# Another list of how many of a step's sums are taken by twos, in a graph-network layer on one core

## The chip, the cores and the metric

The kernel runs on one core of one Trainium2 chip. Its time is the device time of one execution in microseconds; lower is better. A core has a matrix engine (TensorE: PE for its matmuls, PEld for its weight loads), a vector engine (VectorE, DVE), a scalar engine (ScalarE, ACT), GpSimd (POOL) and SyncE (SP), which issues most of the transfers here.

## The reference

The layer normalises nodes, adds up the edges that arrive at each node, and puts both through a two-layer perceptron with a residual. There are N = 12,500 nodes of 128 numbers and 412,500 edges of 48 numbers, sorted by the node that they arrive at.

```
h = maximum(layernorm(x), 0)
agg = segment_sum(edge_attr_48, dst, num_segments=12500)
hid = relu(concat([h, agg, u]) @ W1 + b1)      # u: one row, the same for all nodes
out = x + hid @ W2 + b2
```

All is float32.

## The kernel before, in words

**Edges.** A chunk is 896 edges, 7 on each of 128 partitions, so an edge's number t on its partition runs from 0 to 6. A step takes 8 chunks, in two halves h of 4 chunks; there are 58 steps, the last a shorter one. `load` (L297) fetches two chunks at a time, 336 KB, on SP's queue; `few` (L290) lets five loads be under way and ties a load to TensorE's last issued product. 18 tiles hold edges.

**Sums.** Since the edges are sorted, a chunk's edges arrive at few neighbouring nodes, and its sums go to a window of W = 32 columns. `onehot` (L308) makes on DVE, for a whole step, ones where an edge's node is that of the column. `aggregate` (L334) multiplies: a *position* is one t of one half, so a step has 14 positions. A position can be taken in two ways, and both give the same sums:

- singly: four products, one for each chunk of the half, each with 32 columns of ones as weights and 48 numbers moving through, into 32 partitions of the bank `ps`;
- by twos: two products, each with the 64 columns of two neighbouring chunks as weights and the 96 numbers of both chunks moving through. Half of what that makes (one chunk's ones with the other chunk's edges) is of no use and is never read.

Each product in float32 is two matmuls and two weight loads in the trace. `LEVELS[s]` (L608) says for each step s how many of its 14 positions are taken by twos; L886 deals them out, the second half first and from its last position backwards, so that a step with a level of 1 to 13 begins with single positions and changes once to twos. Where a half has twos, the sums of odd chunks lie 48 numbers further in the bank, and `keep_sums` (L355) copies them on ACT with two more, narrow copies beside the wide one.

**Placing.** `place_columns` (L372, DVE) and `place` (L378, PE, bank `pp`) spread a step's sums over the nodes of its stretch, and `add` (L386, DVE) adds them to `aggT`, two steps after the sums (one step after in the last seven, `LATE`).

**Nodes.** 26 blocks of up to 512 nodes go through `stats`, `root`, `factors`, `normal` (DVE and ACT), `turn` and `keep` (transposed on PE, copied on ACT), `first_h` and `first_a` (first layer, bank `ph`, L468 and L493), `relu` (ACT, tile `hid`, L508), `second` (second layer, bank `po`, L518), `result` (DVE, L527) and `store`. The first five blocks (`FIRST`) are begun early; their half results are kept and added later by `add_h` (L482, DVE). POOL adds the last bias to x (`plus_b2`, L428), clears `aggT` and issues most stores.

**Order.** All is issued by hand, step by step. In step s the loads of step s + 3 go out, then come the pieces of block work that a small planner has given to the step (`piece`, L707), the place of step s − 2, the 14 positions of step s, its copies, its place columns and the ones of step s + 2. The planner does not read `LEVELS`.

Of the kernel before, what the change touches and what calls it, by code (L numbers as in the profile page):

```python
# [22 lines left out]
def kernel(  # L23
# [134 lines left out]
    with fast:  # L158
# [175 lines left out]
        def aggregate(s, h, twos):  # L334
            left = s == NSF and h
            if h == 0:
                banks_s[s] = ps_agg.tile([P, 512], F32, name="ps")[:, :4 * DE].rearrange("p (h f) -> p h f", h=2)
            ps, es, oh = banks_s[s], edges[s], onehots[s]
            n = TT if left else T
            for t in range(n):  # L340
                first, end = t == 0 and h == 0, t == n - 1
                if t >= n - twos:
                    for q in range(0, CH, 2):
                        c = CH * h + q
                        product(ps[W * q:W * (q + 2), h], oh[:, c // 2, t], both[s][c // 2][:, :, t * DE:(t + 1) * DE],
                                start=first, stop=end, skip_group_check=True)
                    continue
                for q in range(1 if left else CH):
                    c = CH * h + q
                    o = DE * (q % 2) if twos else 0  # L350
                    product(
                        ps[W * q:W * (q + 1), h, o:o + DE], oh[:, c // 2, t, c % 2], es[c][:, t * DE:(t + 1) * DE],
                        start=first, stop=end, skip_group_check=True)
# [32 lines left out]
        def add(s):  # L386
            _, v = nc.values_load_multi_w_load_instructions(  # L387
                at_i[0:1, s:s + 1], engines=[DVE], min_val=low(s), max_val=high(s),
                skip_runtime_bounds_check_because="clamped to these on the chip")
            to = aggT[:HI + DE, ds(v[0], WG)]  # L390
            nc.vector.tensor_tensor(to, to, banks_p.pop(s)[:HI + DE, :WG], OP.add)  # L391
# [213 lines left out]
        FLIGHT = 5  # L605


        LEVELS = (0, 0, 0, 0, 7, 0, 0, 9, 14, 3, 14, 14, 0, 14, 3, 3, 2, 0, 5, 14, 0, 14, 2, 3, 0, 4, 14, 0, 14, 2, 4, 0, 3, 0, 5, 14, 0, 14, 0, 4, 0, 2, 0, 3, 14, 0, 14, 4, 2, 2, 0, 2, 2, 4, 0, 0, 0, 0)  # L608
        LATE = NS - 7
        NEAR = len(FIRST) + 1  # L610
        with tc.manual_schedule():
# [242 lines left out]
            for s in range(NS):  # L854
# [27 lines left out]
                if s >= LATE:  # L882
                    for p in now:
                        place(p)
                        add(p)
                twos = [max(0, LEVELS[s] - T), min(T, LEVELS[s])]  # L886
                aggregate(s, 0, twos[0])
# [175 lines left out]
```

## Time and profile before

| | |
|---|---|
| median of 3 runs | 300.32 us (299.75 to 306.59) |
| the profiled execution: time | 298.43 us |
| its span, first to last instruction | 296.6 us |
| TensorE clock granted, mean over the span | 0.991 |
| positions taken by twos | 248 of 809 |
| bytes moved | 95.19 MB |

How to read the rows below: a line of the chain of waits gives a start, a length (both us), and the engine and tile at work, with the number of instructions merged; a line of the timeline gives the same with the operation and its shape, and in square brackets how long the engine had been idle before and what ended that. A shape 128*32 128x48 is a matmul with 128 rows and 32 columns of weights and 48 numbers moving through. Matmuls of one stream overlap, so a timeline length goes a little past the start of the next row.

### The profile page before, as it was taken

How to read it: one execution, taken by the hardware profiler on the slowest of the kernel's cores; microseconds unless marked ns; L12 is line 12 of the kernel's file. 1: busy time of each engine (PE TensorE's matmuls, PEld its weight loads, DVE VectorE, ACT ScalarE, POOL GpSimd, SP SyncE). 2: the span in 40 equal slices, each digit the busy share in tenths (PEclk: the TensorE clock that was granted, in tenths of full speed). 3: DMA queues.
4: the chain of work that ended last, by engine and by line, in shares of the span. 5: the costliest groups of instructions: out<-in, count | busy, mean ns of one | idle time of the engine just before them, and what ended most of it. 6: DMA issues, size and time to landing. Idle time of an engine off the chain costs nothing.

```text
span 296.6 us, 15062 instructions
## 1 busy us (share of the span) xinstructions
PE 283.1 (95%) x6553; PEld 223.5 (75%) x6554; DVE 237.0 (80%) x537; ACT 161.0 (54%) x399; POOL 73.7 (25%) x88
## 2 busy tenths in 40 slices
PE   6799897999999999999999999999999999999992
PEld 2657666898878778878878788867877977787781
DVE  6838969699998997887978699698986799986222
ACT  3477557323756664743666458644651985664420
POOL 3032381130212563021022212021111022103720
PEclk9999998999999999999999999999999999999998
DMA  6999999999999999999999999999999999999962
GB/s 162 372 314 345 272 358 313 370 370 370 356 357 356 326 367 285 298 348 290 332 312 339 346 345 317 336 321 322 310 347 337 353 298 323 337 352 317 363 222 81
DMA packets 69815, 95.19 MB, mean 321 GB/s; under 512 B 5018, under 2 KB 64739, under 8 KB 69743
## 3 DMA queue, kind: packets, MB, share of 16 engines
q1 hardware_dynamic: 67583, 87.66, 89.1%
q0 software_dynamic: 2160, 6.50, 6.1%
q8 instruction: 53, 0.87, 1.2%
q14 instruction: 19, 0.16, 0.1%
HBM read 87.74 MB, written 6.40 MB: 317 GB/s over the span
## 4 chain that ended last, share of the span: by engine, by line
PE 81%; DVE 8%; ACT 3%; DMA 2%; issue 2%; SPq 1%; DVEq 1%
PE ps L195 30%; PE ph L195 21%; PE po L195 14%; PE pp L195 10%; PE pt L199 5%; DVE oh L312 3%; DMA e<-in_edge_attr_dram 2%; DVE place L374 2%; ACT xn L438 1%; ACT hT L452 1%; PE pt L195 1%; DVE st L408 1%; DVE aggT L391 1%; DVE ph L489 1%; DVEq L387 1%
## 5 line engine op out<-in xcount | busy, mean ns | idle before, releaser
L312 DVE TENSOR_TENSOR oh<-iota,rel 128x1792 f32<-128x1792 f32 (+1 forms) x60 | 120.5, 2009 | 0.4 <-ACT rel L270 0.4
L195 PEld LDWEIGHTS ps<-e,oh 128*32 128x32 f32 (+1 forms) x5448 | 94.7, 116 | 21.7 <-issue 5.8
L195 PE MATMUL ps<-e,oh 128*32 128x48 f32 (+1 forms) x5448 | 106.5, 217 | 3.1 <-issue 1.2
L360 ACT COPY sums<-ps 128x192 f32<-128x192 f32 (+2 forms) x129 | 36.7, 285 | 78.7 <-PE ps L195 76.8
L431 POOL TENSOR_TENSOR xb<-xt,b_sb 128x512 f32<-128x512 f32 (+1 forms) x21 | 34.2, 1630 | 131.7 <-DVE aggT L533 79.4
L195 PE MATMUL ph<-hT,w1h 128*128 128x512 f32 (+2 forms) x100 | 49.6, 602 | 0.1
L195 PE MATMUL po<-w,hid 128*128 128x128 f32 (+1 forms) x376 | 48.0, 281 | 0.9 <-ACT hid L516 0.9
L516 ACT ACTIVATE hid<-ph,bias 128x512 f32<-128x512 f32 (+2 forms) x49 | 30.4, 670 | 30.4 <-PE ph L195 22.9
L195 PEld LDWEIGHTS po<-w,hid 128*128 128x128 f32 (+1 forms) x376 | 45.1, 196 | 2.0 <-ACT hid L516 1.3
L391 DVE TENSOR_TENSOR aggT<-aggT,pp 112x246 f32 x58 | 23.6, 406 | 24.5 <-PE pp L195 18.2
L195 PE MATMUL pp<-place,sums 128*112 128x128 f32 x232 | 39.0, 291 | 0.2 <-DVE place L374 0.2
L195 PEld LDWEIGHTS pp<-place,sums 128*112 128x112 f32 x232 | 28.9, 176 | 7.1 <-issue 1.7
L438 ACT ACTIVATE xn<-xt,sh,sc 128x128 f32<-128x128 f32 x80 | 33.1, 483 | 0.3
L374 DVE TENSOR_TENSOR place<-iota,pos 128x256 f32<-128x256 f32 x58 | 32.9, 569 | 0.0
L195 PE MATMUL ph<-aggT,w1a 48*128 48x256 f32 (+1 forms) x192 | 28.6, 402 | 0.2 <-DVE aggT L391 0.2
L195 PEld LDWEIGHTS ph<-aggT,w1a 48*128 48x128 f32 x192 | 17.2, 186 | 10.1 <-issue 6.8
L452 ACT COPY hT<-pt 128x512 f32<-128x512 f32 (+1 forms) x22 | 23.0, 1044 | 3.2 <-PE pt L199 3.1
L195 PEld LDWEIGHTS ph<-hT,w1h 128*128 128x128 f32 x100 | 16.7, 196 | 7.1 <-issue 4.6
L533 DVE TENSOR_TENSOR aggT<-po,xb 128x512 f32<-128x512 f32 x16 | 11.0, 685 | 9.2 <-PE po L195 9.2
L541 POOL DMA_DIRECT2D out_dram<-ot x9 | 5.0, 553 | 51.6 <-DVE ot L533 43.7
L408 DVE BATCH_NORM_STATS2 st<-xt 128x6 f32<-128x128 f32 x80 | 17.3, 277 | 0.0
L199 PE MATMUL pt<-ident,xn 128*128 128x128 f32 x84 | 14.1, 289 | 0.0
(137 smaller groups left out, 188.1 us busy)
## 6 DMA issues: line engine op xcount, KB each, us to landing
e<-in_edge_attr_dram SPq DMA_DIRECT2D x230, 336.0 KB, 5.2
xt<-in_x_dram SPq DMA_DIRECT2D x19, 256.0 KB, 4.9
out_dram<-aggT POOLq DMA_DIRECT2D x16, 256.0 KB, 4.5
out_dram<-ot POOLq DMA_DIRECT2D x7, 256.0 KB, 4.8
di<-in_dst_dram SPq DMA_DIRECT2D x3, 448.0 KB, 5.3
aggT<-in_x_dram SPq DMA_DIRECT2D x4, 256.0 KB, 4.2
xt<-in_x_dram SPq DMA_DIRECT2D x2, 128.0 KB, 4.6
out_dram<-ot SPq DMA_DIRECT2D x2, 128.0 KB, 3.3
```

The source lines that it names most:

```text
L195: last[:] = [nc.tensor.matmul(*a, **k).ins.name]
L199: last[:] = [nc.tensor.transpose(*a, **k).ins.name]
L312: nc.vector.tensor_tensor(to, iota[:, None, :W].to_broadcast([P, n, W]), r[:, :, None].to_broadcast([P, n, W]), OP.is_equal)
L360: nc.scalar.copy(to[k, h], ps[k, h, None, o:o + DE].to_broadcast([k.stop - k.start, h.stop - h.start, 2, DE]))
L374: nc.vector.tensor_tensor(po, iota[:, None, :WP].to_broadcast([P, 2, WP]), pos[:, s, :, None].to_broadcast([P, 2, WP]), OP.is_equal)
L391: nc.vector.tensor_tensor(to, to, banks_p.pop(s)[:HI + DE, :WG], OP.add)
L408: nc.vector.bn_stats(st[:m, q, :], xs[j][:m, q, :])
L431: nc.gpsimd.tensor_tensor(xb[:m, :r], xs[j][:m, :r], b2_sb[:m, None, :].to_broadcast([m, r, D]), OP.add)
L438: nc.scalar.activation(xn[:m, q], xs[j][:m, q], AF.Relu, bias=shift[j][:m, q:q + 1], scale=scale[j][:m, q:q + 1])
L452: nc.scalar.copy(hT[:, :m * r].rearrange("d (p r) -> d r p", r=r), ht[j][:, :m * r].rearrange("d (r p) -> d r p", r=r))
L516: nc.scalar.activation(to, ph, AF.Relu, bias=bias[:, h:h + 1])
L533: nc.vector.tensor_tensor(ot[:m, :r], pos_o[j][:m, :r], xbs[j][:m, :r], OP.add)
```

## The change

One line is replaced: the list `LEVELS`. No other line differs. Over all steps 313 positions in place of 248 are taken by twos.

```
-        LEVELS = (0, 0, 0, 0, 7, 0, 0, 9, 14, 3, 14, 14, 0, 14, 3, 3, 2, 0, 5, 14, 0, 14, 2, 3, 0, 4, 14, 0, 14, 2, 4, 0, 3, 0, 5, 14, 0, 14, 0, 4, 0, 2, 0, 3, 14, 0, 14, 4, 2, 2, 0, 2, 2, 4, 0, 0, 0, 0)
+        LEVELS = (0, 0, 0, 0, 11, 5, 14, 10, 7, 14, 10, 6, 7, 14, 8, 3, 4, 1, 3, 2, 14, 0, 14, 4, 2, 4, 14, 0, 14, 2, 3, 1, 2, 1, 4, 14, 0, 14, 2, 3, 2, 4, 14, 0, 14, 2, 4, 14, 0, 14, 2, 4, 1, 3, 1, 2, 1, 0)
```

Counted by kind, for the steps before the eighth and from it on:

| steps | list | level 0 | levels 1 to 13, and their sum | level 14 |
|---|---|---|---|---|
| 0 to 7 | before | 6 | 2 (16) | 0 |
| 0 to 7 | after | 4 | 3 (26) | 1 |
| 8 to 57 | before | 17 | 21 (64) | 12 |
| 8 to 57 | after | 6 | 32 (105) | 12 |

The instructions of DVE, POOL and SP are the same in number, kind and order. PE has 65 × 2 = 130 products fewer, 260 matmuls and 260 weight loads in the trace's count, and the same number of numbers summed. ACT has two narrow copies beside the wide one in 48 steps in place of 35.

## The prediction

> **What bounds the kernel now.** I read the page's engine table first, then the windows, then the chain of waits.
>
> ```profile
> span 296.6 us, 15062 instructions
> PE 283.1 (95%) x6553; PEld 223.5 (75%) x6554; DVE 237.0 (80%) x537; ACT 161.0 (54%) x399; POOL 73.7 (25%) x88
> ```
>
> PE is busy 95% of the span, but busy matmuls alone need not be a bound. One stretch of the windows (columns: PE, PEld, DVE, ACT, POOL busy us, clock, DMA share, GB/s) settles where it is one:
>
> ```profile
> 60.00:285.00 225.00, 224.84 (x5469) 180.32 (x5468) 188.29 (x417) 126.64 (x316) 54.28 (x56) 1.00 1.00 335
> ```
>
> From 60 to 285 us PE is idle for 0.16 us in all. The waits in that stretch name one matmul of PE that waited, for DVE, and what PE waited for before its sums in the whole run is short and, for edges, early (second fence: us, times):
>
> ```profile
> PE ph L195 <- DVE aggT L391: 0.2, 1, 0.2
> ```
>
> ```profile
>   issue: 1.2, 2
>   DVE st L408: 1.0, 1
>   DMA e<-in_edge_attr_dram: 0.9, 2
> ```
>
> So behind the start PE is one unbroken line of work, and what is added to it is added to the time, unless something in the line had been waiting. The chain of waits, which is PE almost alone there, gives the length of the sums of whole steps:
>
> ```profile
> 119.03 1.64 PE ps L195 x104
> 122.94 1.72 PE ps L195 x100
> 137.46 2.46 PE ps L195 x56
> ```
>
> ```profile
> 127.93 1.33 PE ps L195 x112
> 132.39 1.80 PE ps L195 x96
> ```
>
> A step has 112 matmuls when all 14 positions are single and 4 fewer for each position by twos, so these rows are levels 0 (x112), 2 (x104), 3 (x100), 4 (x96) and 14 (x56). The reader is to see that a position by twos is the dearer one: 1.33 us for 14 single positions, 2.46 for 14 by twos, with half the instructions.
>
> **The price of a level.** Levels 2, 3 and 4 stand at 1.64, 1.72 and 1.80: 0.08 us for each position. Carried back to level 0 this line would give 1.48, and the row has 1.33, so a step that mixes both kinds pays 0.15 once. A full step by twos does not mix: 1.33 + 14 × 0.08 = 2.45, and the row has 2.46. The prices are therefore 1.33 for level 0, 1.48 + 0.08 L for 1 to 13, and 2.46 for 14. Levels 1 and 7 to 11 are estimates from this line.
>
> **Steps 8 to 57: +4.93 us.** The list before has there 17 steps of level 0, 21 mixed ones with 64 positions, and 12 of level 14: 17 × 1.33 + 21 × 1.48 + 64 × 0.08 + 12 × 2.46 = 88.33. The new list has 6, 32 with 105, and 12: 6 × 1.33 + 32 × 1.48 + 105 × 0.08 + 12 × 2.46 = 93.26. Of the +4.93, 3.28 is 41 more positions in mixed steps and 1.65 is 11 more steps that mix (11 × 0.15). Nothing covers this: PE is idle 0.16 us in the stretch. One wait, 0.2 us on DVE, can take up as much of it. **−0.2.**
>
> **Steps 4 to 7.** Here PE does wait, and the timeline of PE shows for what:
>
> ```profile
> 39.79 1.31 PE L195 MATMUL ps<-e,oh 128*32 128x48 f32 x104
> 41.46 0.29 PE L195 MATMUL ps<-e,oh 128*32 128x48 f32 x8 [0.35 <-issue]
> 41.68 0.69 PE L195 MATMUL pp<-place,sums 128*112 128x128 f32 x4
> 42.52 1.23 PE L195 MATMUL po<-w,hid 128*106 128x128 f32 x8 [0.15 <-ACT hid L516]
> 43.68 1.14 PE L195 MATMUL ph<-aggT,w1a 48*128 48x256 f32 x8
> 44.75 1.29 PE L195 MATMUL ps<-e,oh 128*32 128x48 f32 x99
> 46.86 0.37 PE L195 MATMUL ps<-e,oh 128*32 128x48 f32 x13 [0.81 <-issue]
> 47.15 0.69 PE L195 MATMUL pp<-place,sums 128*112 128x128 f32 x4
> 48.62 3.28 PE L195 MATMUL po<-w,hid 128*128 128x128 f32 x16 [0.77 <-ACT hid L516]
> ```
>
> Steps 5 and 6 (at 39.79 and 44.75, level 0) stop in mid stream for 0.35 and 0.81 us with "issue" as the cause: no semaphore, PE had no next instruction. Between the two stops lie 8 + 4 + 8 + 8 + 99 = 127 matmuls, with their weight loads 254 instructions. That is about the size of one packet on the queue that brings instructions:
>
> ```profile
> q8 instruction: 53, 0.87, 1.2%
> ```
>
> 13,107 PE instructions over 53 packets are 247 each. So I read the stops as PE running ahead of its instructions, in the steps that use them up fastest.
>
> New levels 5 and 14 there (before 0 and 0) cost 0.55 and 1.13 on PE, and slow the use of instructions so that both stops should go. It hardly matters, because the po of step 7 at 48.62 waits for ACT's hid, and that for DVE, which lies on the chain from 40 to 48 us with work slowed beside POOL:
>
> ```profile
> 38.99 0.41 DVE L391 TENSOR_TENSOR aggT<-aggT,pp 112x246 f32 x1 [1.71 <-PE pp L195]
> 40.49 3.12 DVE L374 TENSOR_TENSOR place<-iota,pos 128x256 f32<-128x256 f32 x1
> 46.55 1.28 DVE L489 TENSOR_TENSOR ph<-ph,aggT 128x512 f32<-128x512 f32 x2
> ```
>
> ```profile
> 40.14 4.60 POOL L431 TENSOR_TENSOR aggT<-aggT,b_sb 128x512 f32<-128x512 f32 x4
> ```
>
> Worked through: step 4 is longer by 4 × 0.08 = 0.32; step 5 gains 0.55, and loses its stop, which had made its 1.33 some 0.5 longer; step 6 gains 1.13, and loses its stop of about 1.0 (its sums ran from 44.75 to 47.15 at level 0: 2.40 where 1.33 is the price). PE is done with step 6 some 0.4 us later than before, at about 47.5, and still ahead of hid at 48.6. What moves hid is step 4 alone, since DVE's add at 38.99 had waited for PE. **+0.32** (at least 0, if POOL's work then slows DVE for less long; at most 0.32 + 0.4).
>
> **The clock.** Those waits had a consequence:
>
> ```profile
> 45.73:49.14 3.41, 1.82 (x49) 1.45 (x37) 3.41 (x7) 1.87 (x4) 0.37 (x1) 1.00 0.95 313
> 49.14:52.55 3.41, 3.41 (x50) 3.19 (x52) 3.41 (x4) 2.43 (x8) 0.70 (x2) 0.50 0.93 291
> 32.08:35.49 3.41, 2.62 (x72) 2.15 (x74) 3.38 (x8) 1.80 (x3) 0.44 (x1) 1.00 0.93 249
> ```
>
> After a stretch of 3.41 us with PE busy for 1.82, the clock was granted at half for the next 3.41; after one with 2.62 busy it was not. What half the clock cost is seen on the po of step 7 and on step 7's sums (level 9, by the price line 2.20), beside a po at full clock:
>
> ```profile
> 48.62 3.28 PE po L195 x16
> 51.90 2.52 PE ps L195 x76
> 125.28 1.79 PE po L195 x16
> ```
>
> (3.28 − 1.79) + (2.52 − 2.20) = 1.8 us. With the new list PE's sums fill 45.7 to about 47.5 without the stop of 0.81, pp follows, and hid comes at about 48.9, so PE is busy for about 2.5 of the same stretch. That is near the 2.62 that kept the clock, so I take it as kept: **−1.8**; the other end is 0. The Trainium skill, "TensorE: Matmul & The Clock Gate", Part 1, says that half clock follows a window of about 3.4 us in which PE is idle. By that sentence alone the stretch with 1.82 us of work would not have been followed by half clock, and there would be nothing to win here (sum +5.1 in place of +3.3); the trace shows 0.50 after it, so the row decides.
>
> Step 7 goes from 9 to 10: **+0.08**.
>
> **What is costed at nothing.** ACT's narrow copies rise from 71 to some 97:
>
> ```profile
> L360 ACT COPY sums<-ps 32x96 f32<-32x96 f32 x45 | 10.3, 230 | 1.0
> L360 ACT COPY sums<-ps 32x192 f32<-32x192 f32 x26 | 8.1, 310 | 0.6
> ```
>
> About 26 × 0.27 = 7 us more on an engine that is busy 126.64 of 225; the sums are placed two steps later, and in the last seven steps behind a block's po or ph of about 2 us, while two copies last 0.5. If that cover went, `place` would be late by up to 0.5 us in each of three steps. Transfers are paced by PE and only get more room. The 130 fewer products save nothing of their own, since their price is in the rows of whole steps.
>
> **The sum.** −0.2 + 4.93 + 0.32 − 1.8 + 0.08 = **+3.3** on the profiled execution's 298.43 gives 301.8 us; with half clock kept, +5.1 gives 303.6. The profiled execution is 1.89 below the median of the runs shown, and below their fastest, so part of that lies on any unprofiled run. I add half of it and predict **302.8 us**, 0.8% over the median.
>
> **Rivals.**
>
> *Half clock stays* (or comes at another place of the start): 303.6 + 0.95 = 304.5 us. For it: 2.5 us of work lies between the two rows, and the place of the 3.41 us stretches is not the kernel's to choose. Chance 0.25.
>
> *Instructions run out in other places.* The stops of 0.35 and 0.81 came in dense single steps, and which 256 instructions hold such a step shifts with the list. For it: every new mixed level of 1 to 3 leaves a step nearly as dense as level 0. Against it: 260 matmuls fewer over a longer time. Six stops of 0.8 on the forecast give 307.6 us; it is decided above 306.3, that is from five such stops, or from two with another half-clock stretch of 1.8. Chance 0.20.
>
> *Not slower: the dense steps pay in the other runs.* The other executions of before took 1.3 to 8.2 us more than the profiled one. If that is PE running out of instructions in some of its 23 steps of level 0, the new list with 10 such steps has less of it. Then after comes to the sum without the addition, 301.8, or with the stops of the start gone from the chain too, 300, against a before that is measured at up to 306.6. It decides for "not slower" when before's usual run loses 3.4 us or more so. Against it: the profiled execution has no stop between 60 and 285 us. Chance 0.12.
>
> *The change does nothing, because loads set the pace.* For it, SP's queue, which mostly waits for landings:
>
> ```profile
> SPq L144 <- DMA e<-in_edge_attr_dram: 108.2, 176, 2.4
> ```
>
> Then dearer positions only fill waits, and the time is 298.4 − 1.8 + 1 to 300.3: about 299 us. Against it: PE waited for edges twice in the whole run, 0.9 us together. Chance 0.05.
>
> **How the numbers follow.** The forecast has the remaining 0.38. A difference within 2% is about what a measurement of this kernel can tell from no change: 294.3 to 306.3 us. Slower by more than that: the 0.20 of the instructions and 0.05 of the half clock (two such stretches). Faster by more: 0.05, out of the third rival, where before is measured high. Within: 0.70. For 8 in 10 the range leaves out the loads' case, the better half of the third, and the worse half of the second: 300.2 to 306.8. The forecast's own range, from the bounds of its terms, is 301.4 to 304.1.
>
> **What would show it.** The chain of the changed kernel: level-14 steps at 2.46, level 1 at 1.56, level 10 at 2.28; ps rows of 128*64 x1252. PE busy again without a gap from about 60 us. No "issue" between 39 and 48 us. The po after step 6 at 1.79, not 3.28, and no clock of 0.50 near 49. The prediction is wrong if PE shows idle time behind 60 us (then another thing bounds it, or instructions ran out), or if a position by twos comes at another price than 0.08.

## The result, and the profile after

| | before | after |
|---|---|---|
| executions | 8 | 8 |
| median, and range | 303.16 us (299.75 to 308.55) | 303.35 us (302.50 to 304.71) |
| profiled execution, and its span | 298.43 / 296.6 us | 303.00 / 301.2 us |
| mean clock granted in it | 0.991 | 0.993 |

The ratio of after to before is 1.0131, with a 95% interval of 1.0087 to 1.0176: slower, by less than 2%. It leaves out disturbed executions, and its value is what three of after's (303.64, 303.92 and 304.30 us) give over before's 299.75 and 300.32; over all eight on either side the means are equal (303.52 and 303.48 us). So the size leans on before's quicker executions. In the four later measurements of before, on other occasions, its 40 executions have a median of 301.3 us, 0.7% under after's. The two profiled executions differ by 4.57 us.

The page of the changed kernel, first the span and the engines, then what PE spent of the chain that ended last, by engine:

```profile
span 301.2 us, 14566 instructions
PE 288.7 (96%) x6293; PEld 228.7 (76%) x6294; DVE 233.3 (77%) x537; ACT 168.3 (56%) x425; POOL 78.1 (26%) x88
...
PE 90%; DMA 4%; ACT 1%; SPq 1%; DVE 1%; issue 1%; POOL 0%
```

PE does 260 matmuls fewer and is busy 5.6 us longer. To see where that lies, take one window from the first product of step 8 to the first of step 57, in before and then in after (columns as in the prediction: PE, PEld, DVE, ACT and POOL busy, clock, DMA share, GB/s):

```profile
56.03:281.66 225.63, 225.47 (x5463) 181.33 (x5461) 190.94 (x418) 127.65 (x318) 52.55 (x53) 1.00 1.00 335
```

```profile
55.78:286.04 230.26, 230.26 (x5299) 185.04 (x5298) 189.64 (x418) 133.51 (x340) 57.42 (x54) 1.00 0.99 327
```

PE is busy throughout in both: 0.16 us idle before, none after. The stretch is 4.63 us longer, and that is the whole difference of the profiled executions: after starts step 8 at 55.78 us, before at 56.03 (−0.25), and what follows step 57 takes 15.13 us in place of 14.94 (+0.19). The chain of waits shows the prices of the new levels:

```profile
162.07 1.56 PE ps L195 x108
...
51.89 2.28 PE ps L195 x72
...
115.06 1.33 PE ps L195 x112
118.72 2.46 PE ps L195 x56
```

Level 1 (x108) is 1.56 and level 10 (x72) 2.28, as the price line had them; levels 0 and 14 are where they were. A position by twos costs 0.08 us, and no wait absorbs it.

The start has another shape though the same length. PE's timeline of after around steps 3 to 7, to be read beside the one in the prediction:

```profile
31.98 0.60 PE L195 MATMUL pp<-place,sums 128*112 128x128 f32 x4
33.69 0.57 PE L195 MATMUL po<-u,w1u 64*128 64x1 f32 x4 [1.11 <-DMA u<-L_gnn_graph_globals_dram]
34.20 3.99 PE L195 MATMUL ps<-e,oh 128*32 128x48 f32 x68
...
41.38 1.95 PE L195 MATMUL ps<-e,oh 128*32 128x48 f32 x92
...
46.95 2.53 PE L195 MATMUL ps<-e,oh 128*64 128x96 f32 x56
49.41 0.69 PE L195 MATMUL pp<-place,sums 128*112 128x128 f32 x4
49.94 1.95 PE L195 MATMUL po<-w,hid 128*128 128x128 f32 x16
```

No "issue" stands in steps 5 and 6 any more, and the po of step 7 takes 1.95 us in place of 3.28: both as forecast. But step 4 takes 3.99 where level 11 has the price 1.48 + 11 × 0.08 = 2.36. The windows say why:

```profile
30.77:34.19 3.42, 2.14 (x13) 1.39 (x12) 3.32 (x7) 2.46 (x5) 1.05 (x2) 1.00 1.02 283
34.19:37.60 3.41, 3.41 (x59) 3.29 (x60) 2.47 (x4) 0.00 (x0) 0.49 (x1) 0.50 1.06 335
```

The half clock of before at 49 us is gone, and another one has come at 34.2 us. Ahead of it PE waited for u, the row of globals, whose transfer took 5.35 us in place of before's 4.6. Steps 0 to 3 are the same in both lists, so the new levels cannot have caused that wait; e1 and e7 below, with the old list there, wait for u too (0.8 and 2.2 us).

### The profile page after: what moved, and what is told of

Read it like the earlier page. It is cut to its first block, busy times and chain, and to the rows that moved or that the text cites. A ratio compares the mean times of both kernels' runs of the same rounds, so it can differ in the third digit from the quotient of the medians.

```text
span 301.2 us, 14566 instructions
## 1 busy us (share of the span) xinstructions
PE 288.7 (96%) x6293; PEld 228.7 (76%) x6294; DVE 233.3 (77%) x537; ACT 168.3 (56%) x425; POOL 78.1 (26%) x88
## 4 chain that ended last, share of the span: by engine, by line
PE 90%; DMA 4%; ACT 1%; SPq 1%; DVE 1%; issue 1%; POOL 0%
PE ps L195 36%; PE ph L195 22%; PE po L195 15%; PE pp L195 11%; PE pt L199 5%; DMA e<-in_edge_attr_dram 2%; DMA u<-L_gnn_graph_globals_dram 2%; PE pt L195 1%; ACT hT L452 1%; DVE oh L312 1%; SPq L144 0%; SPq L398 0%; ACT sums L360 0%; POOL w1u L549 0%; ACT aggT L480 0%
## 5 line engine op out<-in xcount | busy, mean ns | idle before, releaser
L195 PEld LDWEIGHTS ps<-e,oh 128*32 128x32 f32 (+1 forms) x5188 | 101.2, 118 | 20.8 <-issue 4.6
L195 PE MATMUL ps<-e,oh 128*32 128x48 f32 (+1 forms) x5188 | 114.3, 220 | 1.7 <-DMA e<-in_edge_attr_dram 1.7
L360 ACT COPY sums<-ps 128x192 f32<-128x192 f32 (+3 forms) x155 | 43.5, 281 | 85.3 <-PE ps L195 82.8
L431 POOL TENSOR_TENSOR xb<-xt,b_sb 128x512 f32<-128x512 f32 (+1 forms) x21 | 38.7, 1842 | 130.4 <-DVE aggT L533 90.6
L195 PE MATMUL po<-w,hid 128*128 128x128 f32 (+1 forms) x376 | 46.9, 277 | 0.8 <-ACT hid L516 0.8
L195 PEld LDWEIGHTS po<-w,hid 128*128 128x128 f32 (+1 forms) x376 | 44.1, 191 | 1.9 <-ACT hid L516 1.0
L374 DVE TENSOR_TENSOR place<-iota,pos 128x256 f32<-128x256 f32 x58 | 29.0, 502 | 0.0
```

Of the source, the lines that this page charges most:

```text
L195: last[:] = [nc.tensor.matmul(*a, **k).ins.name]
L360: nc.scalar.copy(to[k, h], ps[k, h, None, o:o + DE].to_broadcast([k.stop - k.start, h.stop - h.start, 2, DE]))
L374: nc.vector.tensor_tensor(po, iota[:, None, :WP].to_broadcast([P, 2, WP]), pos[:, s, :, None].to_broadcast([P, 2, WP]), OP.is_equal)
L431: nc.gpsimd.tensor_tensor(xb[:m, :r], xs[j][:m, :r], b2_sb[:m, None, :].to_broadcast([m, r, D]), OP.add)
```

## The experiments

The first theory was the one on record: the price of PE, plus a start that varies. Its open point was the rival of the instructions, since the new list had not met it. The rival theory: PE's instructions come in packets of 256, a list has to fit the places where packets end, and the profiled execution of before was free of stops only because its list fits.

**Halves of the change.** Two kernels take one half of the new list each, and a third sets all levels to 0.

```
e1_old_start   LEVELS = before[:8] + after[8:]
e2_new_start   LEVELS = after[:8] + before[8:]
e3_no_twos     LEVELS = (0,) * 58
```

> The new list from step 8 on, the old one in steps 0 to 7. If a position by twos costs only its PE price (0.08 us, 0.15 for a step that mixes), this is the profiled execution of before with +4.9 us in steps 8 to 57: about 303 us, PE without idle time behind 60 us. If PE's instructions come in packets of 256 and a list must fit the places where these end, moving the later steps by 24 positions (192 instructions) against the list that they were in spoils the fit: stops in mid stream named issue, 10 or more of 0.3 to 1 us behind 60 us, and 308 to 316 us. A list by the loads (third idea) would give no change from before, 300 us.

> The old list from step 8 on, the new one in steps 0 to 7 (24 more positions by twos there). PE price alone: the two stops of 0.35 and 0.81 us in steps 5 and 6 go, 2.1 us of work come, and the span is that of before within 1 us, about 299 us. Instruction packets: 192 instructions fewer ahead of step 8 put the old list out of its place; 5 to 12 stops of 0.2 to 1 us, 302 to 306 us.

> No position by twos at all. PE price alone: 22 us fall away in steps 8 to 57 and 2 before, 275 us. Loads as the bound: PE waits for edges (DMA named before ps), 285 to 295 us. Instruction packets: 992 more PE instructions than before in less time, a stop named issue at nearly every packet, 30 of 0.5 to 3 us, and 298 to 312 us, no better than before though PE has 24 us less work.

| kernel | median, range (us) | ratio to before, 95% interval | steps 8 to 57 |
|---|---|---|---|
| e1_old_start | 308.59 (307.33 to 311.58) | 1.0254 (1.0164 to 1.0344) | 235.35 |
| e2_new_start | 313.17 (308.90 to 316.71) | 1.0374 (1.0304 to 1.0444) | 238.02 |
| e3_no_twos | 321.76 (318.45 to 325.52) | 1.0625 (1.0537 to 1.0713) | 252.62 |

The same window by steps, for e2 (the work of before) and e1 (the work of after):

```profile
53.81:291.83 238.02, 229.73 (x5463) 183.45 (x5461) 189.95 (x418) 127.93 (x318) 51.49 (x54) 1.00 0.97 321
```

```profile
54.52:289.87 235.35, 231.94 (x5299) 185.89 (x5298) 190.86 (x418) 133.43 (x340) 52.32 (x55) 1.00 0.97 322
```

With the same 5463 matmuls, e2 takes 12.4 us more than before; with the same 5299, e1 takes 5.1 more than after. PE is idle for 8.3 and 3.4 us in stretches that were full. What PE waited for in the whole run (us in total, times, longest), in e2, e1 and e3:

```profile
PE ps L195 <- issue: 6.7, 9, 1.7
```

```profile
PE ps L195 <- issue: 5.0, 6, 1.5
```

```profile
PE ps L195 <- issue: 31.4, 36, 2.0
...
PE ps L195 <- DMA e<-in_edge_attr_dram: 1.6, 3, 0.9
```

It is mostly "issue": waits for edges come to 2.7, 2.3 and 1.6 us, where before has 0.9 and after 1.7. So neither half of the new list is harmful by itself; it is the join that matters. And e3 shows how large the thing is: by the price line its steps 8 to 57 have 50 × 1.33 = 66.5 us of sums, 26.8 less than after's 93.26, and they take 22.4 us more (in its slowest execution, the profiled one; its quickest took 7 us less). Its timeline shows where PE stops:

```profile
104.34 0.84 PE L195 MATMUL ps<-e,oh 128*32 128x48 f32 x58 [0.76 <-issue]
105.11 0.69 PE L195 MATMUL pp<-place,sums 128*112 128x128 f32 x4
105.63 1.02 PE L195 MATMUL ph<-hT,w1h 128*128 128x512 f32 x2
106.59 1.14 PE L195 MATMUL ph<-aggT,w1a 48*128 48x256 f32 x8
107.66 0.66 PE L199 MATMUL pt<-ident,xn 128*128 128x128 f32 x4
108.24 1.40 PE L195 MATMUL ps<-e,oh 128*32 128x48 f32 x112
109.57 0.69 PE L195 MATMUL pp<-place,sums 128*112 128x128 f32 x4
110.10 1.95 PE L195 MATMUL po<-w,hid 128*128 128x128 f32 x16
111.98 0.70 PE L195 MATMUL ps<-e,oh 128*32 128x48 f32 x45
114.06 0.96 PE L195 MATMUL ps<-e,oh 128*32 128x48 f32 x67 [1.37 <-issue]
```

From the stop at 104.34 to the one at 114.06 are 58 + 4 + 2 + 8 + 4 + 112 + 4 + 16 + 45 = 253 matmuls, and as many weight loads: 506. With PE's own waiting instructions, which these rows leave out, the trace has 512 from the one to the other: two packets. Between them one packet's end was crossed without a stop. Counted in the trace from PE's first instruction, every stop named "issue" in these runs, before's two in steps 5 and 6 among them, resumes at number 193 or 194 of a 256. In steps 8 to 57 PE resumes 1.2 to 1.6 us after a packet of the instruction queue has landed, and 3.7 to 7.0 us after it had passed the same number of the 256 before, having used up those 256 in 3.1 to 5.4 us. The page's row of that queue in after, 0.84 MB in 51 packets, makes 16.5 KB each, 64 bytes for each of 256 instructions:

```profile
q8 instruction: 51, 0.84, 1.1%
```

**Shift the list without changing it.** Products of one column are put into the start, behind a wait of PE that was to hide them; they feed nothing that is read.

```
             spare()
+            ph = ps_h.tile([P, 512], F32, name="ph")
+            for i in range(24):      # e4, on before;  16 in e7, on e1
+                product(ph[:, i:i + 1], ones, iota[:, 0:1], start=True, stop=True)
```

> The list of before, unchanged; 24 products of one column each are added behind the second warming product, in time in which PE waits for the first edges, so that all later PE instructions lie 96 further on. Their results are overwritten and never read. PE price alone: the time of before within 1 us, since the work behind 8 us is the same. Instruction packets: the same steps now meet the ends of packets elsewhere, 10 to 20 stops named issue of 0.2 to 1.3 us behind 60 us, 305 to 315 us.

> The kernel with the new list from step 8 on and the old one before it, which had stops, with 16 products of one column added behind the second warming product (64 PE instructions; results overwritten and never read). 192 + 64 = 256, so the steps from 8 on meet the ends of packets where they do in the changed kernel. Instruction packets: the stops behind 60 us go, and the time falls from 308.6 to 302 to 304 us by adding work. PE price alone: no change from that kernel, 308 us.

e4_shifted took 311.14 us (308.08 to 313.45), ratio 1.0231 (1.0143 to 1.0318). Its steps 8 to 57, in its slowest execution, which is the profiled one:

```profile
61.49:296.18 234.69, 228.21 (x5463) 182.63 (x5461) 190.07 (x418) 127.56 (x318) 51.89 (x54) 1.00 0.97 319
```

The same work is stretched by 9.1 us, 6.5 of it idle. One thing was wrong: the added products were not free. Step 8 starts 5.5 us later, so by this run alone it could be the time of the steps and not the count of instructions; e8_new_weights_early below, which shifts the time alone, speaks against that.

e7_old_start_64 puts the 64 instructions back that e1 is short of a whole packet (192 + 64 = 256). It took 306.64 us (303.91 to 307.55), ratio 1.0261 (1.0029 to 1.0492); the time is not better than e1's beyond doubt, since the added products cost some 3 us at the start. The stretch answers:

```profile
57.69:290.25 232.56, 231.25 (x5299) 185.55 (x5297) 189.65 (x418) 133.85 (x340) 63.35 (x55) 1.00 0.98 325
```

PE's idle time there falls from 3.41 to 1.31 us, and the stretch from 235.35 to 232.56; after has 230.26. More than half of the loss is undone by a shift, not all.

**A whole packet fewer, the decisive run.** Before's list from step 8, with 32 more positions by twos ahead of it. That is 256 instructions fewer; e2 had 24 more, 192 fewer.

```
before          steps 4 to 7:   7,  0,  0,  9
e2_new_start    steps 4 to 7:  11,  5, 14, 10
e11_start_256   steps 4 to 7:   7, 13, 14, 14
e12_start_256b  steps 4 to 7:  14, 14, 14,  6
```

> The list of before from step 8, and 7, 13, 14, 14 in place of 7, 0, 0, 9 in steps 4 to 7: 32 more positions by twos, so 256 PE instructions fewer ahead of step 8, one whole packet (e2_new_start had 24 more, 192 instructions fewer, and cost 12.4 us in the same steps 8 to 57). If the place of the instructions modulo 256 decides: steps 8 to 57 take the 225.6 us of before again (at most 226.5), no stop of more than 0.3 us behind 60 us, the stops in steps 5 and 6 go, and the time is that of before within 2 us, 297 to 300 for the profiled execution (PE's 2.6 us for 32 positions fall mostly into its wait for hid in step 7). Rival: what decides is how many instructions are used per microsecond, or at what time of the run a dense step comes. Then this list, denser than that of after and with its steps moved in time like those of e2_new_start, takes 308 to 314 us, with 8 to 16 stops behind 60 us.

> The same 32 positions more, dealt as 14, 14, 14, 6 in steps 4 to 7. If the place modulo 256 decides, steps 8 to 57 take 225.6 to 226.5 us as in e11_start_256, though the steps ahead of them are of other lengths and step 8 starts 0 to 1.5 us later; the time is 298 to 301 us. Rival, by rate or by time: 308 to 314 us, and not the same as e11_start_256.

e11_start_256 took 301.69 us (298.76 to 304.93), ratio 0.9999 (0.9949 to 1.0049); e12_start_256b took 300.81 us (297.01 to 303.65), ratio 0.9961 (0.9912 to 1.0011). Both are equal to before, while e2, with 8 positions fewer, is 3.74% slower. Steps 8 to 57 in e11 and e12:

```profile
56.66:286.76 230.10, 227.30 (x5463) 181.89 (x5461) 189.91 (x418) 128.56 (x319) 60.31 (x54) 1.00 0.99 328
```

```profile
54.41:284.29 229.88, 226.67 (x5463) 181.83 (x5461) 190.15 (x418) 127.71 (x318) 63.25 (x54) 1.00 1.00 331
```

The expected 225.6 to 226.5 was missed: both profiled executions (303.81 us in e11, 300.80 in e12) have 230, with 2.8 and 3.2 us of idle time, of which the waits show these in e12:

```profile
PE ps L195 <- DMA e<-in_edge_attr_dram: 2.8, 6, 0.7
PE pt L199 <- issue: 1.8, 1, 1.8
```

The one stop of e12 and the three of e11 all resume at number 194 of a 256. For e12's, and for two of e11's, the packet began 3.4 to 4.2 us after PE had crossed the end before it; over all packets of the stretch the median is 1.8 us in e11 and 1.2 in e12, and 9 in 10 are at most 2.7. So place decides the large part (e2's 12.4 us become 4.3 to 4.5), and a late packet now and then costs 0.6 to 1.8 us even in a list that fits.

**Dense lists that fit.** If place were all, a list with far fewer twos, but with every packet's end put into slow work, would win. Four lists were planned so:

```
e5_locked     79 positions by twos:  14 in steps 5, 9, 11; 2 to 5 in 10 others
e6_locked_b   80:  14 in steps 5, 9; 5 to 8 in 4 others; 1 to 3 in most that have any, 4 in step 53
e9_fit_87     87:  14 in steps 9, 10; 12 in step 5; 0 to 5 elsewhere
e10_fit_more  151:  14 in steps 9, 23, 25, 46, 47; 13 in step 5; 0 to 9 elsewhere
```

> A third list, worked out from the traces: 79 positions by twos, 65 of them in steps 8 to 57, placed so that the end of every 256 PE instructions falls where it is asked for long before it is needed. PE price alone: PE has 16 us less to do than in before, about 282 us. Instruction packets: the same 282 us, with stops only where a packet takes longer than 6 us, 0 to 5 of them; 281 to 285 us. Loads as the bound: PE waits for edges, DMA named before ps, 288 to 297 us.

> The same idea with 80 positions by twos, spread over more steps, which leaves each packet about 0.5 us more and costs 0.8 us more on PE. Instruction packets: 282 to 285 us, stops 0 to 3. Loads as the bound: the same 288 to 297 us as the other one.

> 87 positions by twos (75 from step 8 on), placed with an exact count of PE's instructions this time, so that by the step prices of before each packet's end leaves 6.2 us or more for the 300 instructions ahead of it, as in before. PE has 12 us less to do than in before. If only the place of the packets' ends counts: 284 to 288 us. If packets come no faster than one in about 5 us whatever the place (50 packets behind 56 us here, 44 in before), stops feed on each other and it takes 300 to 320 us, as the two lists before it did.

> 151 positions by twos (138 from step 8 on), with 6.6 us or more for the 300 instructions ahead of each packet's end. PE has 6 us less to do than in before. Place alone: 290 to 293 us, so 2 to 3% faster than before. One packet in about 5 us: 48 packets behind 56 us, 296 to 305 us.

| kernel | median, range (us) | ratio to before, 95% interval | steps 8 to 57 | matmuls in them |
|---|---|---|---|---|
| e5_locked | 320.94 (319.41 to 323.85) | 1.0781 (1.0521 to 1.1042) | 249.05 | 6130 |
| e6_locked_b | 320.32 (316.61 to 322.05) | none was given | 245.64 | 6127 |
| e9_fit_87 | 312.10 (306.47 to 317.86) | none was given | 236.50 | 6091 |
| e10_fit_more | 308.20 (305.77 to 309.37) | 1.0207 (1.0119 to 1.0294) | 236.57 | 5839 |

All four missed. In e5 and e6 the plan left PE's own waiting instructions out of the count, so that its places drift (steps 8 to 57 have 103 of them); e9 and e10 count them. PE waited for its instructions still, in e9 and in e10:

```profile
PE ps L195 <- issue: 12.7, 14, 1.9
...
PE pp L195 <- issue: 2.1, 1, 2.1
```

```profile
PE ps L195 <- issue: 5.6, 7, 1.5
PE po L195 <- issue: 3.3, 2, 1.7
```

What they share is a rate. With each matmul and its weight load as two instructions, 256 of them took in steps 8 to 57: in e3 252.62 / (6391 × 2 / 256) = 5.06 us, in e5 5.20, in e6 5.13, in e9 4.97, in e10 5.19; before, without a stop there, 5.29, and after 5.56. So packets came about every 5 us on average, though single ones began only 3.4 to 3.6 us after the one before; before runs almost at this average, and after keeps about half a microsecond from it. The plans did not come true in the traces either: at the stops of e9 and e10 PE had used up its 256 instructions in 4.1 to 5.2 us, where the plan had 6.2 us or more for 300, which is 5.3 for 256. None of the four bears out the rival that a list can be made much denser by fitting it; that no list can is not shown.

**The start.** The transfers that PE waited for at 33.7 us are asked for two half steps, that is one step, earlier.

```
-            at(6, load_weights_of_sums)
+            at(4, load_weights_of_sums)
```

> The changed kernel with the weights of the first layer's third part asked for two half steps earlier, so that PE's wait of 1.4 us for them at 32 us goes. If the half clock at 34 to 38 us came from that wait, the clock is full there, step 4's sums take 2.4 us and not 3.7, and the time falls by 1 to 2.5 us, to about 301.5. If the first 50 us are set by DVE anyway, the time stays within 0.5 us of 303.3.

e8_new_weights_early took 303.45 us (302.07 to 305.63), ratio 1.0164 (0.9959 to 1.0369): nothing that can be told from after. The wait for u is gone, and the loss has moved:

```profile
31.77 0.62 PE L195 MATMUL ps<-e,oh 128*32 128x48 f32 x37 [1.17 <-issue]
...
35.86 0.60 PE L195 MATMUL po<-u,w1u 64*128 64x1 f32 x4 [0.73 <-ACT hT L452]
36.39 4.01 PE L195 MATMUL ps<-e,oh 128*32 128x48 f32 x68
```

PE now stops for instructions at 31.77, waits for hT at 35.86, and step 4 takes 4.01 us, at half clock as in after. It starts 2.2 us later than in after.

That delay makes e8 a test of time against count: PE has the same matmuls in the same order as in after, and as many instructions, and all from step 4 on comes 2.2 to 2.4 us later. Its steps 8 to 57 have no stop:

```profile
57.99:288.46 230.47, 230.36 (x5299) 185.08 (x5298) 190.10 (x418) 133.31 (x340) 53.90 (x54) 1.00 0.98 326
```

The traces of the other runs also show the start with either list and with half clock at either place (us from the span's start; "half clock" is when the stretch of half clock in the start began):

| kernel | list in steps 0 to 7 | half clock | product with u | step 8 | between |
|---|---|---|---|---|---|
| e4_shifted | before's | none | 41.56 | 61.49 | 19.93 |
| e7_old_start_64 | before's | 37.99 | 37.51 | 57.69 | 20.18 |
| e1_old_start | before's | 35.17 | 34.14 | 54.52 | 20.38 |
| before | before's | 49.14 | 33.96 | 56.03 | 22.07 |
| after | after's | 34.19 | 33.69 | 55.78 | 22.09 |
| e8_new_weights_early | after's | 36.42 | 35.86 | 57.99 | 22.13 |
| e2_new_start | after's | 32.92 | 31.67 | 53.81 | 22.14 |

(e8 has one more such stretch, at 22.77.) Half clock in step 4 is the usual thing: in 11 of the 14 profiled executions such a stretch begins between 32 and 39 us, with either list. In ten of them it begins within 1.4 us of the product with u, which had waited for u or for hT; in e3 it follows a stop for instructions. Before's execution is not one of the 11.

## Why the prediction was right or wrong

**The price of a level: right.** Forecast for steps 8 to 57 +4.93, less 0.2 for the wait on DVE; measured 225.63 to 230.26, +4.63 against +4.73. The rows of levels 1 and 10, which before did not have, came as estimated.

**Costed at nothing: right.** ACT's narrow copies did rise, to 97, and nothing in steps 8 to 57 waited, since PE is busy for all of the 230.26 us.

**Steps 4 to 7: right in kind.** The stops of steps 5 and 6 went with the longer steps. The new levels were to cost 0.32 + 0.08, since PE would still wait for hid in step 7. In after it does not wait there; it waits for hid once, 0.77 us, ahead of step 6. Between runs with half clock in step 4 (after, e2 and e8 against e1 and e7) the new levels cost 1.7 to 2.0 us. So the cover that the forecast counted on was not there. No run has after's start at full clock, so how it would be there is open.

**The clock: this step failed.** "I take it as kept: −1.8". The half clock at 49 us did go, and po came back from 3.28 to 1.95. But 3.99 − 2.36 = 1.6 us of it came again in step 4, behind 2.14 us of work in 3.42, and from the product with u to step 8 after takes 22.09 us where before took 22.07: of the −1.4 that the start was to bring (0.32 − 1.8 + 0.08), nothing came. Two things failed. The forecast took one execution's half clock at 49 us for the kernel's, where nearly every other trace has it in step 4. And it took about 2.5 us of work in 3.41 for enough because 2.62 had kept the clock. The other traces show that this is no rule: in e12 half clock follows a stretch with 2.54 us of work, and, 55 stretches of 3.413 us later, full clock one with 1.85.

```profile
29.39:32.80 3.41, 2.54 (x25) 1.95 (x27) 3.10 (x6) 2.21 (x4) 0.75 (x2) 1.00 0.83 244
32.80:36.22 3.42, 3.42 (x48) 3.34 (x44) 2.43 (x3) 0.00 (x0) 0.00 (x0) 0.50 1.03 309
...
217.12:220.53 3.41, 1.85 (x101) 1.73 (x101) 1.11 (x1) 0.28 (x1) 0.00 (x0) 1.00 0.93 250
220.53:223.95 3.42, 3.42 (x46) 2.63 (x42) 2.58 (x3) 2.30 (x7) 0.00 (x0) 1.00 0.90 288
```

So PE's busy time in a stretch does not say whether half clock follows; what does is open. The Trainium skill, "TensorE: Matmul & The Clock Gate", Part 1, ties half clock to an idle window of about 3.4 us; the trace again shows 0.50 behind a window that was 63% busy. The rival of the half clock at another place of the start, at 303.6 us for the profiled execution, is the one that came, at 303.0; that the loss in step 4 left the start as long as before's at 49 us (22.09 against 22.07) is luck.

**The likeliest outcome: this failed too.** The forecast was "no change" in the sense of within 2%, taken as about what a measurement can tell. The ratio on record tells 1.31% from nothing, with an interval of less than half a per cent to either side; against before's later executions it is some 0.7%, in the same direction. The sum itself was 1.1%, with the half clock kept 1.7%, and nearly all of it was PE's price without cover: by its own rows the prediction should have named a small loss as likeliest.

**The addition of 0.95: right by accident.** 302.8 us is near the measured 303.35, but the sum without it, 301.8, lacked the 1.4 us that the start did not save.

**Instructions in other places: a near miss.** The rival with 0.20 did not come in after, and the argument against it was the wrong one. "260 matmuls fewer over a longer time" holds as much for e1, which has after's list from step 8 and 5.0 us of stops in sums. (One bound of this rival is a shade off: two stops of 0.8 and a half clock of 1.8 on 302.8 give 306.2, not above 306.3.) What kept after free of them is that its list fits its own start; half of it joined to half of the other list loses 5 to 12 us.

**Dense steps that pay in the other runs.** It lost, but something speaks for its mechanism: after's executions lie within 2.2 us, before's within 8.8, and before uses its instructions nearly as fast as they came in any run. That before's slower executions are ones with late packets was not seen, since of before only one execution, a quick one, has a trace.

**Open.** What begins half clock, if not the share of busy time; why PE used the instructions of e9 and e10 faster than the plan had it; what makes one packet start 4 us late (the transfers beside it were not varied). Of the 4.3 us by which e12's stretch is longer than before's, 3.0 are more idle time and 1.2 more busy time of PE, and why that rose is not known.

## What to carry to other kernels

An edit that trades fewer instructions for more work on the bounding engine is worth only what the supply of instructions was costing there: look for idle time whose cause is "issue", count the engine's instructions between two such stops, its waiting ones included, and if it is a multiple of 256, the place and the rate of instructions are part of the schedule. Where such a kernel has been fitted, an insertion or removal ahead of it that is not a whole packet can cost more (5 to 12 us here) than the edit is worth, so test halves of a change with the count kept. And before a lost clock is booked as a gain, look in a second trace whether the kernel loses it at the same place: here one execution had it at 49 us and nearly all others at 32 to 39.

## What the runs showed of the hardware

- PE's instructions came in packets of 256 (16.5 KB), on average one in about 5 us beside the loads of this kernel (4.97 to 5.20 us in the five kernels that stopped most for them; single ones began 3.4 to 3.6 us apart); PE resumed 1.2 to 1.6 us after a packet had landed.
- Taking all twos away left 26.8 us less work by the price line and made the kernel 6.25% slower (1.0537 to 1.0713 in the ratio): fewer but longer products were the quicker ones. Of that kernel's steps 8 to 57 PE was idle for 31.0 us, and its waits named "issue" before sums are 31.4 us in the whole run.
- Many stops went with half clock: e3 and e5, with the most of them, had a mean clock of 0.96 and 0.97 in steps 8 to 57; e2 and e4, with 9 each there, had 1.00, as the kernels without.
- Half clock followed 3.41 us stretches with up to 2.54 us of matmuls (e12), and full clock one with 1.85: the busy share alone did not decide it.
